# Splitting fp32 operands on ScalarE straight from PSUM, gates by tanh, and a three-pass product with W^T, in a gated GNN followed by graph attention

## The chip, the core and the metric

The kernel runs on one core of a Trainium2 chip. The metric is the device time of that core in microseconds, the median of several runs. The core has a matrix engine (TensorE, PE in the profile; PEld is its weight load), a vector engine (VectorE, DVE), a scalar engine (ScalarE, ACT), GpSimd (POOL) and a queue that issues transfers (SyncE, SP). Matmuls write to PSUM, eight banks of 128 x 512 fp32; everything else is in SBUF.

## The reference

There are 64 graphs of 256 nodes with 256 features. Each graph has its own 256 x 256 adjacency matrix. Two layers are computed:

```
h  = relu(layernorm(x))                 # layer 0
for i in 0..2:
    aggr = A^T (h weight[i])            # A = (adj != 0)
    gi, gh = aggr w_ih^T + b_ih, h w_hh^T + b_hh
    r, z = sigmoid(i_r + h_r), sigmoid(i_z + h_z)
    n = tanh(i_n + r * h_n)
    h = (1 - z) * n + z * h
x  = x + h
h  = relu(layernorm(x))                 # layer 1
g  = h W^T
e  = leaky(g a_left [rows] + g a_right [columns]); masked where adj == 0
x  = x + softmax(e) g
```

## The kernel before, in words

Two graphs make a pair, and there are 32 pairs. The features of a pair lie as two tiles of 128 features x 512 (two graphs of 256 nodes), so the moving operand of a gate matmul is 128 x 512. Each pair goes through three GRU steps (i = 0, 1, 2) and then the attention.

**Precision by splitting.** The gate products are done in float32r, which keeps fewer mantissa bits than fp32. Both operands are split: a value v into a top part v0 (the leading bits) and a remainder v1, and a third tile d that combines the two. The weights' three factors are made once in the setup, by `factors`, into `fac` tiles (`hh` for w_hh; 0, 1, 2 for weight[i] w_ih^T). The moving operands are split at each step by `split` (L445): a VectorE operation that masks off low bits into a fp32 tile t (the cut, L322), a ScalarE copy of t to float32r (L449), a VectorE subtraction v - t (L450), and a VectorE scalar_tensor_tensor for d (L451).

**A gate** (L455) takes one PSUM bank. Its top part adds two float32r products per operand block (L464). ScalarE then scales the bank by 1 + 1/4096 and adds a bias (L478), and the rest adds the third product (L469). A step has six gates: r, z (each from h and from the aggregate), nh (from h) and ni (from the aggregate), each for two blocks of 128 outputs. That is 72 matmuls a step, 216 a pair.

**A step.** The state hT is split into h0, h1. The propagation with A, prop (L584), is eight matmuls of 128 x 256 for each feature block. ScalarE copies its bank into SBUF (L588), and `split` makes g from the copy. Then come the gates: r and z by ScalarE's sigmoid (L599, L610), u = nh * r (L603), u += ni (L606), n by tanh (L607), and h = n + z * (h - n) by three VectorE operations (L615 to L617). For the next propagation h goes back to node-major form by a DMA transpose and a gather on SP (L489, L494), a ScalarE copy that joins 16-bit halves (L502), and a split into hi and lo (L641, L642). In the last pair TensorE transposes instead (L631).

**Attention.** After a second layernorm and relu, the two dot products with a are taken on VectorE (L656) by va, a W prepared in the setup. One of them is spread over the columns by TensorE (L667), Prelu makes the leaky scores (L671), a predicated copy masks them (L674), and a reduction takes the maximum (L676). The four exp instructions of both graphs follow as one operation (L683). The weights are turned by DMA as above (L705, L706; by TensorE in the last pair, L700). Then mix (L714) multiplies them with the features in plain fp32, ScalarE copies the bank to SBUF (L718), and project (L723) multiplies with W^T, plain fp32, four matmuls of 128 x 256 a graph. VectorE divides by the softmax sum and adds the residual (L728), and SP stores (L731).

**The order.** The order of instructions on each engine is written out by a planner (`Plan`) when the kernel is built. Every operation has an engine, an assumed duration, the tiles that it reads and writes, and a priority from a due time less a hand-set lead (`LEAD`, by operation name). The planner places one operation after the other by the time at which it could start, then by priority. Tiles come from slot classes (28 "full", 32 "round", 8 "bank" and so on), and an operation that needs a new tile must wait for a free slot. At most four pairs are in work at once. Each engine works in its order; semaphores keep the dependencies.

Of the kernel before, what the change touches and what calls it, by code (L numbers as in the profile page):

```python
# [27 lines left out]
    "w load": 28000, "w copy": -12000, "w cut": -5000, "w 1": -17000, "w copies": -7000, "G": -9000, "G copy": -5400,  # L28
    "va copy": 4000, "in 0 stats": 5000, "in 1 relu": 10000, "turn copy 0": -11800, "h0 0": 17000, "h0 d": 13000,
    "h1 0": 36000, "prop 0": 11200, "g0 cut": 3000, "g1 cut": 13000, "g1 0": -28000, "r 0 topT": 51000,  # L30
    "r 0 rest": -4300, "r 0": 29000, "ni 0 rest": 46000, "z 0 topF": -48000, "z 0": 11000, "d mul 0": -19000,
    "r 1 topT": -34000, "r 1 rest": -1000, "nh 1 topF": -42000, "nh 1 scale": -38000, "nh 1 rest": 3000,
    "ni 1 topF": -24000, "tanh 1": 10000, "z 1 topF": -61000, "z 1 scale": -112000, "z 1": 6000, "back 0": -36000,
    "hi 0": 28000, "back copy 1": -67000, "hi 1": 52000, "mid 0 stats": -14000, "right 0": -8000,
    "mid 1 eps": -23000, "mid 1 relu": 9000, "dot 1": -31000, "mix 0": -28000, "p copy 1": 40000,
    "project 1": -6000, "turn 1 gather": 2000,
# [16 lines left out]
class Plan:  # L53
# [6 lines left out]
    def __init__(self, window, lead):  # L60
        self.ops, self.slots, self.window, self.pair = [], {}, window, -1
        self.writer, self.readers = {}, {}
        self.due = None
        self.stage = None
        self.lead = lead
        self.keep = {"full": 0, "round": 0}
# [4 lines left out]
    def op(self, name, eng, occ, lat, fn, r=(), w=(), ahead=0, port=False):  # L71
# [3 lines left out]
        o.stage, o.name, o.lead = self.stage, name, self.lead.get(name, 0)  # L75
# [125 lines left out]
def tile_gated_gnn_then_gat(  # L201
# [34 lines left out]

    nc = tc.nc
# [16 lines left out]
    plan.slot_class("full", [const.tile([P, GN], F32, name=f"full{i}") for i in range(28)])  # L254
# [37 lines left out]
    C = 1.0 / SPLIT  # L292

# [4 lines left out]
    b_rz = const.tile([P, EB], F32, name="b_rz")  # L298
    b_i = vec[:, 2 * DB : 2 * DB + EB]
# [3 lines left out]
    wT = const.tile([P, DB, D], F32, name="wT")  # L303
# [21 lines left out]
    def setup():  # L325
# [16 lines left out]
        dve("b_rz", 70, lambda: nc.vector.tensor_add(b_rz, b_i, b_h), r=[("vec", ONE)], w=[("b_rz", ONE)])  # L342

# [10 lines left out]
        def transposed(dst, region, blocks):  # L354

            def go_for(c):
                pt = Buf("bank")

                def go():
                    for r, (b, k) in enumerate(blocks):  # L360
                        nc.tensor.transpose(pt.t[:, ts(r, P)], parts(b)[:, k, ts(c, P)], ident)

                n = len(blocks)
                pe("w turn", TR * n, go, r=[(b, ONE) for b, _ in blocks] + [("ident", ONE)], w=[(pt, ONE)])
                act("w copy", 140 + n * 110, lambda: nc.scalar.copy(dst(c), pt.t[:, : n * P]), r=[(pt, ONE)], w=[region(c)])

            for c in range(DB):
                go_for(c)

        H = E3 // 2  # L370

        def factors(m, T):

            def one(kb, half):
                f = lambda j: fac[m][:, j, kb, ts(half, H)]
                b, t = T[kb][half], Buf("full")
                src, top = lambda: b.t[:, :H], lambda: t.t[:, :H]
                key = (f"fac{m}", ((kb, half),))
                cut("w cut", top, src, H, [(b, ONE)], [(t, ONE)])
                dve2("w 1", 460, lambda: nc.vector.tensor_sub(src(), src(), top()), r=[(t, ONE)], w=[(b, ONE)])  # L380

                def copies():
                    nc.scalar.copy(f(0), top())
                    nc.scalar.activation(f(1), src(), AF.Copy, scale=SPLIT)

                act("w copies", 800, copies, r=[(b, ONE), (t, ONE)], w=[(f"fac{m}", ((kb, half, 0),))])
                dve2("w d", 510, lambda: nc.vector.scalar_tensor_tensor(f(2), top(), -C, src(), op0=ALU.mult, op1=ALU.add),
                    r=[(b, ONE), (t, ONE)], w=[(f"fac{m}", ((kb, half, 1),))])

            for half in range(2):  # L390
                for kb in range(DB):
                    one(kb, half)
# [4 lines left out]
        def whole(T, blocks):  # L397
            for half in range(2):
                transposed(lambda c, half=half: T[c][half].t[:, :H], lambda c, half=half: (T[c][half], ONE),
                           blocks[3 * half : 3 * half + 3])  # L400
# [4 lines left out]
        whole(whhT, whh_n)  # L405
# [24 lines left out]
        transposed(lambda c: wT[:, c, :], lambda c: ("wT", (c,)), W_n)  # L430
# [12 lines left out]
    WT = [("wT", (0, 1))]  # L443

    def split(name, v):  # L445

        t, v0, v1, vd = Buf("full"), Buf("round"), Buf("round"), Buf("round")
        cut(name + " cut", lambda: t.t, lambda: v.t, GN, [(v, ALL)], [(t, ONE)])
        act(name + " 0", C512, lambda: nc.scalar.copy(v0.t, t.t), r=[(t, ONE)], w=[(v0, ONE)])  # L449
        dve2(name + " 1", V512, lambda: nc.vector.tensor_sub(v1.t, v.t, t.t), r=[(v, ALL), (t, ONE)], w=[(v1, ONE)])  # L450
        dve2(name + " d", V512, lambda: nc.vector.scalar_tensor_tensor(vd.t, v1.t.bitcast(F32), -SPLIT, t.t, op0=ALU.mult, op1=ALU.add),  # L451
            r=[(v1, ONE), (t, ONE)], w=[(vd, ONE)])
        return v0, v1, vd

    def gate(name, e, terms, tops, apart=False, bias=0.0):  # L455
# [22 lines left out]
        act(name + " scale", 575 if "nh" in name else A512, lambda: nc.scalar.activation(bank.t, bank.t, AF.Identity, bias=bias, scale=1.0 + C),  # L478
# [4 lines left out]
    def dma_turn(name, src, t, gathers):  # L483
# [5 lines left out]
        plan.op(name, "SP", 1370, 3500, lambda: nc.sync.dma_start_transpose(  # L489
# [6 lines left out]
        for region, dst, blocks in gathers:  # L496
            plan.op(name + " gather", "SP", 1320, 4300 if blocks == slice(None) else 3100, lambda dst=dst, blocks=blocks: gather(dst, blocks),
                    r=[(t, ALL)], w=[region])
# [10 lines left out]
    def norm_relu(name, src, dst):  # L509
# [11 lines left out]
        dve(name + " stats", 995, stats, r=[(src, ALL)], w=[(sm, (0, 1))])  # L521
# [13 lines left out]
    def pair(p):  # L535
        plan.pair = p

# [33 lines left out]
        for i in range(L):  # L571
# [4 lines left out]
            for db in range(DB):  # L576
                pa, ag = Buf("bank"), Buf("full")
# [10 lines left out]
                act(f"prop copy {db}", A512, lambda pa=pa, ag=ag: nc.scalar.copy(ag.t, pa.t), r=[(pa, ONE)], w=[(ag, ALL)])  # L588
                gs.append(split(f"g{db}", ag))
# [5 lines left out]
            for db in range(DB):  # L595
# [3 lines left out]
                act(f"r {db}", 575, lambda b=r_, k=pr, db=db: nc.scalar.activation(b.t, k.t, AF.Sigmoid, bias=b_rz[:, db : db + 1]),  # L599
                    r=[(pr, ONE), ("b_rz", ONE)], w=[(r_, ONE)])  # L600
                en = 2 * DB + db
                ph = gate(f"nh {db}", en, [("hh", hs)], tops, bias=b_h[:, en : en + 1])
                dve(f"u {db}", V512, lambda u=u, k=ph, b=r_: nc.vector.tensor_mul(u.t, k.t, b.t),  # L603
                    r=[(ph, ONE), (r_, ONE)], w=[(u, ONE)])
# [6 lines left out]
                    b.t, k.t, AF.Sigmoid, bias=b_rz[:, DB + db : DB + db + 1]),  # L611
# [4 lines left out]
                dve2(f"d mul {db}", V512, lambda d=d, b=z_: nc.vector.tensor_mul(d.t, d.t, b.t), r=[(z_, ONE)], w=[(d, ALL)])  # L616
                dve2(f"d add {db}", V512, lambda u=u, d=d: nc.vector.tensor_add(d.t, d.t, u.t), r=[(u, ONE)], w=[(d, ALL)])  # L617
# [31 lines left out]
        for g in range(G):  # L649
# [20 lines left out]
            for nb in range(NB):  # L670
                act(f"leaky {g}", 365, lambda b=sc[g], nb=nb, pR=pR, sm=sm: nc.scalar.activation(  # L671
                    parts(b)[:, nb, :], pR.t[:, :N], AF.Prelu, bias=sm.t[:, 12 + nb : 13 + nb], alpha=LEAKY_SLOPE),
                    r=[(pR, ONE), (sm, (12 + nb,))], w=[(sc[g], (nb,))])
# [5 lines left out]
        def exps():  # L679
            for g in range(G):  # L680
                s = sms[g].t
                for k in range(NB):
                    nc.scalar.activation(parts(pm_[g])[:, k, :], parts(pm_[g])[:, k, :], AF.Exp, bias=s[:, k : k + 1],  # L683
                                         accum_out=s[:, 4 + k : 5 + k])

        plan.op("exps", "ACT", 4 * 490 + 2600, 4 * 490 + 1300 + 200, exps, r=[(s, ONE) for s in sms],
                w=[(b, ALL) for b in pm_] + [(s, (1,)) for s in sms])

        for g in range(G):
# [3 lines left out]
            pT, pg, ag, pv = Buf("full"), Buf("bank"), Buf("full"), Buf("bank")  # L693
# [24 lines left out]
            act(f"mix copy {g}", A512, lambda ag=ag, pg=pg: nc.scalar.copy(ag.t, pg.t), r=[(pg, ONE)], w=[(ag, ONE)])  # L718

            def project(ag=ag, pv=pv):  # L720
                for ib in range(NB):
                    for db in range(DB):
                        nc.tensor.matmul(pv.t[:, ts(ib, D)], ag.t[:, db * N + ib * P : db * N + (ib + 1) * P],  # L723
                                         wT[:, db, :], start=(db == 0), stop=(db == DB - 1))

            pe(f"project {g}", 4 * MM, project, r=[(ag, ONE)] + WT, w=[(pv, ONE)])
# [41 lines left out]
```

## Time and profile before

| what | value |
| --- | --- |
| median of 3 runs | 2126.16 us (2124.05 to 2127.03) |
| profiled execution | 2126.64 us |
| its span, first to last instruction | 2124.9 us |
| mean granted TensorE clock | 0.991 |
| L464 and L469 (gates) | 6912 matmuls |
| L584 (prop) | 1536 matmuls of 256 columns |
| L714 (mix), L723 (project) | 512 records each, for 256 instructions |
| table loads on ScalarE | 65, 1283 ns each |
| L502 (join), ScalarE | 310 copies, 1172 ns |
| L478 (gate scale), ScalarE | 768, 592 or 665 ns |

How to read the profile: a row of the groups names line, engine, operation, output<-input by tile names, shapes and count; then the busy time of the group, the mean of one in ns, and the idle time of the engine just before its members with what ended it. A matmul's mean is longer than the distance between two starts, since matmuls overlap. The chain is the work that ended last, followed back from the end: at each point what released the next piece. "issue" is time in which nothing visible was waited for. A wait row reads: engine and line that waited, engine and line waited for, total us, times, longest.

### The profile page before, as it was taken

What the parts mean: (1) busy time and instruction counts of PE and PEld (TensorE: products, weight loads), DVE (VectorE), ACT (ScalarE), POOL (GpSimd) and SP (SyncE); (2) the same over time, 40 slices, a digit from 0 to 9 for tenths busy, and PEclk for the clock granted to TensorE, in tenths of its full rate; (3) what the DMA queues carried; (4) which work ended last, traced back from release to release, by engine and by line L of the source; (5) the groups of instructions that cost most, each with busy time, mean ns of one, the idle gap of its engine ahead of it and who ended that gap; (6) DMA issues with size and microseconds to landing.
All of it is one profiled execution on the core that took longest, in us unless ns stands there. A gap on an engine that the chain in (4) does not pass through costs nothing.

```text
span 2124.9 us, 31090 instructions
## 1 busy us (share of the span) xinstructions
PE 2084.8 (98%) x9737; PEld 1712.9 (81%) x9737; DVE 1780.2 (84%) x4148; ACT 1892.6 (89%) x3255; POOL 142.9 (7%) x198
## 2 busy tenths in 40 slices
PE   8999999999999999999999999999999999999997
PEld 6787888888888888888888888888888888888875
DVE  7787888888888888888888888888888888888775
ACT  7788999999998999998999999999999989999865
POOL 1000000000000000000000000000000000000000
PEclk9999999999999999999999999999999999999998
DMA  3456765656765546766546665556765657665531
GB/s 99 75 105 119 139 117 104 103 108 127 135 118 97 107 110 129 134 119 96 109 110 129 132 120 101 104 112 127 134 118 97 108 108 131 130 119 90 91 59 40
DMA packets 729254, 234.35 MB, mean 110 GB/s; under 512 B 660977, under 2 KB 729089, under 8 KB 729089
## 3 DMA queue, kind: packets, MB, share of 16 engines
q1 hardware_dynamic: 729056, 232.36, 58.0%
q8 instruction: 77, 1.26, 0.3%
q14 instruction: 89, 0.72, 0.1%
q10 hardware_dynamic: 32, 0.01, 0.0%
HBM read 52.96 MB, written 16.78 MB: 33 GB/s over the span
## 4 chain that ended last, share of the span: by engine, by line
PE 78%; ACT 9%; DMA 6%; SPq 3%; DVE 2%; issue 2%; ACTq 0%; DVEq 0%
PE bank L464 39%; PE bank L469 19%; PE bank L584 7%; PE bank L714 6%; DMA full<-full 5%; PE bank L723 5%; SPq L494 3%; ACT full L502 2%; ACT bank L478 2%; ACT full L683 1%; ACT round L449 1%; ACT L683 1%; PE bank L421 1%; PE bank L667 1%; ACT full L599 0%
## 5 line engine op out<-in xcount | busy, mean ns | idle before, releaser
L464 PE MATMUL bank<-round,fac 128*128 128x512 f32 x2304 | 624.1, 399 | 1.9 <-ACT round L449 1.7
L464 PE MATMUL bank<-round,fac_hh 128*128 128x512 f32 x2304 | 617.9, 397 | 3.7 <-ACT round L449 3.6
L464 PEld LDWEIGHTS bank<-round,fac_hh 128*128 128x128 f32 x2304 | 432.8, 189 | 105.8 <-ACT round L449 4.8
L464 PEld LDWEIGHTS bank<-round,fac 128*128 128x128 f32 x2304 | 431.9, 189 | 101.8 <-ACT round L449 2.1
L478 ACT ACTIVATE bank<-bank 128x512 f32<-128x512 f32 x576 | 339.6, 592 | 48.3 <-PE bank L464 46.1
L502 ACT COPY full<-full 128x1024 uint16<-128x1024 uint16 x310 | 363.2, 1172 | 20.8 <-DMA full<-full 15.5
L469 PE MATMUL bank<-round,fac_hh 128*128 128x512 f32 x1152 | 356.2, 399 | 2.4 <-ACT bank L478 1.9
L469 PE MATMUL bank<-round,fac 128*128 128x512 f32 x1152 | 356.5, 396 | 0.5 <-ACT bank L478 0.5
L450 DVE TENSOR_TENSOR round<-full,full 128x512 fp32r<-128x512 f32 x384 | 255.2, 684 | 1.7
L469 PEld LDWEIGHTS bank<-round,fac 128*128 128x128 f32 x1152 | 214.4, 188 | 51.1 <-ACT bank L478 2.9
L469 PEld LDWEIGHTS bank<-round,fac_hh 128*128 128x128 f32 x1152 | 208.4, 189 | 57.6 <-ACT bank L478 16.6
L451 DVE SCALAR_TENSOR_TENSOR round<-round,full 128x512 fp32r<-128x512 f32 x384 | 252.2, 682 | 0.9 <-PE bank L464 0.5
L449 ACT CAST round<-full 128x512 fp32r<-128x512 f32 x384 | 239.5, 631 | 8.5 <-DVE full L322 5.6
L603 DVE TENSOR_TENSOR full<-bank,full 128x512 f32<-128x512 f32 x192 | 131.8, 687 | 114.2 <-ACT full L599 107.9
L524 POOL TENSOR_TENSOR small<-small,nhalf 128x2 f32<-128x2 f32 x128 | 106.2, 839 | 1787.7 <-DVE small L522 1785.5
L584 PEld LDWEIGHTS bank<-round,round 128*128 128x128 f32 x1536 | 206.1, 190 | 17.9 <-DVE round L642 2.7
L584 PE MATMUL bank<-round,round 128*128 128x256 f32 x1536 | 217.2, 287 | 3.4 <-DVE round L642 1.9
L610 ACT ACTIVATE full<-bank,b_rz 128x512 f32<-128x512 f32 x192 | 131.7, 687 | 88.8 <-PE bank L469 88.7
L615 DVE TENSOR_TENSOR full<-full,full 128x512 f32<-128x512 f32 x192 | 132.2, 689 | 75.2 <-ACT full L607 71.9
L322 DVE TENSOR_SCALAR full<-full 128x512 int32<-128x512 int32 (+1 forms) x400 | 163.7, 418 | 17.2 <-ACT full L588 8.8
L616 DVE TENSOR_TENSOR full<-full,full 128x512 f32<-128x512 f32 x192 | 131.8, 688 | 42.6 <-ACT full L610 41.9
L478 ACT ACTIVATE bank<-bank,vec 128x512 f32<-128x512 f32 x192 | 127.7, 665 | 13.1 <-PE bank L464 13.0
(78 smaller groups left out, 2407.6 us busy)
## 6 DMA issues: line engine op xcount, KB each, us to landing
full<-full SPq DMA_DIRECT2D x496, 128.0 KB, 3.5
x<-in_x_dram SPq DMA_DIRECT2D x64, 256.0 KB, 3.3
adj<-in_adj_dram SPq DMA_DIRECT2D x64, 256.0 KB, 3.1
full<-in_x_dram SPq DMA_DIRECT2D x64, 256.0 KB, 3.0
out_dram<-full SPq DMA_DIRECT2D x64, 256.0 KB, 2.4
full<-full SPq DMA_DIRECT2D x248, 64.0 KB, 2.2
full<-full SPq DMA_TRANSPOSE x310, 3.1
full<-in_L_gnn_w_ih_dram SPq DMA_DIRECT2D x3, 256.0 KB, 2.8
```

What stands on the lines that cost most here:

```text
L322: dve2(name, 60 + n * 0.54, lambda: nc.vector.tensor_scalar(dst().bitcast(I32), src().bitcast(I32), CUT, None, op0=ALU.bitwise_and), r=r, w=w)
L449: act(name + " 0", C512, lambda: nc.scalar.copy(v0.t, t.t), r=[(t, ONE)], w=[(v0, ONE)])
L450: dve2(name + " 1", V512, lambda: nc.vector.tensor_sub(v1.t, v.t, t.t), r=[(v, ALL), (t, ONE)], w=[(v1, ONE)])
L451: dve2(name + " d", V512, lambda: nc.vector.scalar_tensor_tensor(vd.t, v1.t.bitcast(F32), -SPLIT, t.t, op0=ALU.mult, op1=ALU.add), r=[(v1, ...
L464: nc.tensor.matmul(bank.t, f(m, j, kb), b.t, start=(first and n == 0), stop=True, skip_group_check=True)
L469: nc.tensor.matmul(bank.t, f(m, 2, kb), s[kb][2].t, start=False, stop=True, skip_group_check=True)
L478: act(name + " scale", 575 if "nh" in name else A512, lambda: nc.scalar.activation(bank.t, bank.t, AF.Identity, bias=bias, scale=1.0 + C), ...
L502: act(name, 1065, lambda: nc.scalar.copy(dst.t.bitcast(U16).rearrange("p (j n b) -> p j n b", j=2, b=2), src.t.bitcast(U16).rearrange(f"p ...
L584: nc.tensor.matmul(pa.t[:, ts(g, N)], b, parts(A[g])[:, sb, :], start=(n == 0), stop=(n == len(terms) - 1))
L603: dve(f"u {db}", V512, lambda u=u, k=ph, b=r_: nc.vector.tensor_mul(u.t, k.t, b.t), r=[(ph, ONE), (r_, ONE)], w=[(u, ONE)])
L615: dve2(f"d sub {db}", V512, lambda u=u, d=d: nc.vector.tensor_sub(d.t, d.t, u.t), r=[(u, ONE)], w=[(d, ALL)])
L616: dve2(f"d mul {db}", V512, lambda d=d, b=z_: nc.vector.tensor_mul(d.t, d.t, b.t), r=[(z_, ONE)], w=[(d, ALL)])
```

## The change

- **Split without a cut.** `split` no longer masks bits into a tile t. ScalarE multiplies v by 1 - 1/8192 and rounds to float32r in one pass, giving v0; VectorE subtracts v0 from v, then makes d from v0 and v1. For g the source is the PSUM bank of the propagation itself, so the ScalarE copy to SBUF is gone, and the bank is read by ScalarE and then by VectorE.
- **r and z by tanh.** sigmoid(y) = (1 + tanh(y/2)) / 2. The factors of one half go into scaled biases, into the n rows of w_hh (halved as they are copied in the setup) and into VectorE operations that become scalar_tensor_tensor.
- **Project in float32r.** W^T gets three factors in the setup. The mix bank is split as g is. Project becomes eight float32r matmuls, a ScalarE scale of its bank, and four more.
- **exps** becomes one planner operation for each graph.
- **Planner.** The slots of class full go from 28 to 26. The leads are other ones, the first and the last pair may have their own, and a few assumed durations are changed.

```diff
-    "project 1": -6000, "turn 1 gather": 2000,
...
+    "right 0": -20000, "dot 1": 9000, "p copy 1": -65000, "c1 d": -31000, "last h0 0": 10000, "last dot 1": -17000,
...
-    plan.slot_class("full", [const.tile([P, GN], F32, name=f"full{i}") for i in range(28)])
+    plan.slot_class("full", [const.tile([P, GN], F32, name=f"full{i}") for i in range(26)])
...
+    BELOW = 1.0 - C / 2
...
-    wT = const.tile([P, DB, D], F32, name="wT")
+    fac["W"] = const.tile([P, 3, DB, D], F32R, name="fac_W")
...
-    def split(name, v):
-
-        t, v0, v1, vd = Buf("full"), Buf("round"), Buf("round"), Buf("round")
-        cut(name + " cut", lambda: t.t, lambda: v.t, GN, [(v, ALL)], [(t, ONE)])
-        act(name + " 0", C512, lambda: nc.scalar.copy(v0.t, t.t), r=[(t, ONE)], w=[(v0, ONE)])
-        dve2(name + " 1", V512, lambda: nc.vector.tensor_sub(v1.t, v.t, t.t), r=[(v, ALL), (t, ONE)], w=[(v1, ONE)])
-        dve2(name + " d", V512, lambda: nc.vector.scalar_tensor_tensor(vd.t, v1.t.bitcast(F32), -SPLIT, t.t, op0=ALU.mult, op1=ALU.add),
-            r=[(v1, ONE), (t, ONE)], w=[(vd, ONE)])
+    def split(name, v, bank=False):
+
+        v0, v1, vd = Buf("round"), Buf("round"), Buf("round")
+        act(name + " 0", A512 if bank else C512, lambda: nc.scalar.activation(v0.t, v.t, AF.Copy, scale=BELOW), r=[(v, ALL)], w=[(v0, ONE)])
+        (dve if bank else dve2)(name + " 1", V512, lambda: nc.vector.tensor_sub(v1.t, v.t, v0.t.bitcast(F32)),
+                                r=[(v, ALL), (v0, ONE)], w=[(v1, ONE)])
+        dve2(name + " d", V512, lambda: nc.vector.scalar_tensor_tensor(
+            vd.t, v1.t.bitcast(F32), -SPLIT, v0.t.bitcast(F32), op0=ALU.mult, op1=ALU.add),
+            r=[(v0, ONE), (v1, ONE)], w=[(vd, ONE)])
...
-                act(f"prop copy {db}", A512, lambda pa=pa, ag=ag: nc.scalar.copy(ag.t, pa.t), r=[(pa, ONE)], w=[(ag, ALL)])
-                gs.append(split(f"g{db}", ag))
+                gs.append(split(f"g{db}", pa, True))
...
-                act(f"r {db}", 575, lambda b=r_, k=pr, db=db: nc.scalar.activation(b.t, k.t, AF.Sigmoid, bias=b_rz[:, db : db + 1]),
+                act(f"r {db}", 575, lambda b=r_, k=pr, db=db: nc.scalar.activation(
+                    b.t, k.t, AF.Tanh, bias=b_rz[:, db : db + 1], scale=0.5),
...
-                dve(f"u {db}", V512, lambda u=u, k=ph, b=r_: nc.vector.tensor_mul(u.t, k.t, b.t),
-                    r=[(ph, ONE), (r_, ONE)], w=[(u, ONE)])
+                dve(f"u {db}", S512, lambda u=u, k=ph, b=r_: nc.vector.scalar_tensor_tensor(
+                    u.t, b.t, 1.0, k.t, op0=ALU.add, op1=ALU.mult), r=[(ph, ONE), (r_, ONE)], w=[(u, ONE)])
...
-                dve2(f"d mul {db}", V512, lambda d=d, b=z_: nc.vector.tensor_mul(d.t, d.t, b.t), r=[(z_, ONE)], w=[(d, ALL)])
-                dve2(f"d add {db}", V512, lambda u=u, d=d: nc.vector.tensor_add(d.t, d.t, u.t), r=[(u, ONE)], w=[(d, ALL)])
+                dve2(f"d mul {db}", V512, lambda d=d, b=z_: nc.vector.scalar_tensor_tensor(
+                    d.t, b.t, 1.0, d.t, op0=ALU.add, op1=ALU.mult), r=[(z_, ONE)], w=[(d, ALL)])
+                dve2(f"d add {db}", V512, lambda u=u, d=d: nc.vector.scalar_tensor_tensor(
+                    d.t, d.t, 0.5, u.t, op0=ALU.mult, op1=ALU.add), r=[(u, ONE)], w=[(d, ALL)])
...
-        plan.op("exps", "ACT", 4 * 490 + 2600, 4 * 490 + 1300 + 200, exps, r=[(s, ONE) for s in sms],
-                w=[(b, ALL) for b in pm_] + [(s, (1,)) for s in sms])
+            act(f"exps {g}", 2 * 497, exps, r=[(sms[g], ONE)], w=[(pm_[g], ALL), (sms[g], (1,))])
...
-            act(f"mix copy {g}", A512, lambda ag=ag, pg=pg: nc.scalar.copy(ag.t, pg.t), r=[(pg, ONE)], w=[(ag, ONE)])
-
-            def project(ag=ag, pv=pv):
-                for ib in range(NB):
-                    for db in range(DB):
-                        nc.tensor.matmul(pv.t[:, ts(ib, D)], ag.t[:, db * N + ib * P : db * N + (ib + 1) * P],
-                                         wT[:, db, :], start=(db == 0), stop=(db == DB - 1))
-
-            pe(f"project {g}", 4 * MM, project, r=[(ag, ONE)] + WT, w=[(pv, ONE)])
+            cs = split(f"c{g}", pg, True)
+
+            def project(js, first, cs=cs, pv=pv):
+                for n, (ib, db, j) in enumerate((ib, db, j) for ib in range(NB) for db in range(DB) for j in js):
+                    nc.tensor.matmul(pv.t[:, ts(ib, D)], cs[j].t[:, db * N + ib * P : db * N + (ib + 1) * P],
+                                     fac["W"][:, j, db, :], start=(first and n == 0), stop=True, skip_group_check=True)
+
+            pe(f"project {g}", 8 * PROP, lambda project=project: project((0, 1), True),
+               r=[(cs[0], ONE), (cs[1], ONE), ("facW", ((0, 0), (1, 0)))], w=[(pv, ONE)])
+            act(f"project {g} scale", A512, lambda pv=pv: nc.scalar.activation(pv.t, pv.t, AF.Copy, scale=1.0 + C), w=[(pv, ONE)])
+            pe(f"project {g} rest", 4 * PROP, lambda project=project: project((2,), False),
+               r=[(cs[2], ONE), ("facW", ((0, 1), (1, 1)))], w=[(pv, ONE)])
```

## The prediction, made before the result was known

> **What bounds the kernel now.** I read the page's busy line first, then the busy time in three stretches, then TensorE's waits in the middle stretch, then the rows that give the price of one instruction, then the chain that ended last. Busy line of the page and the three stretches (columns: length, then PE, PEld, DVE, ACT, POOL busy, granted clock, DMA share, GB/s):
>
> ```profile
> PE 2084.8 (98%) x9737; PEld 1712.9 (81%) x9737; DVE 1780.2 (84%) x4148; ACT 1892.6 (89%) x3255; POOL 142.9 (7%) x198
> ...
> 0.00:200.00 200.00, 185.54 (x818) 145.93 (x819) 153.88 (x343) 162.42 (x292) 14.51 (x26) 0.96 0.51 105
> 200.00:2000.00 1800.00, 1790.73 (x8446) 1480.51 (x8445) 1546.39 (x3613) 1647.39 (x2816) 125.37 (x168) 1.00 0.61 115
> 2000.00:2125.00 125.00, 108.55 (x476) 86.51 (x474) 79.94 (x194) 82.83 (x149) 3.00 (x4) 0.92 0.30 55
> ```
>
> TensorE is busy 1790.7 of the middle 1800 us; it idles 9.3 us there, 14.5 us in the head and 16.5 us in the tail. A busy TensorE need not be at its peak, so I checked by counting: the middle holds 6094 gate matmuls (L464 and L469), at 216 a pair 28.2 pairs, 63.8 us a pair. A pair's work at the pitches read below is 216 x 0.2325 (gates, start to start in the timeline) + 48 x 0.118 (prop, L584) + 32 x 0.217 (mix and project records) + 4 x 0.11 (L667) = 63.3 us. So TensorE runs at its own pace, and ScalarE (91%) and VectorE (86%) are slack there. Its waits in the middle:
>
> ```profile
> PE bank L714 <- ACT full L502: 7.8, 14, 1.3
> PE bank L469 <- ACT bank L478: 1.0, 3, 0.5
> ```
>
> Only 9 us can be won by ending waits in the middle; the rest must come out of TensorE's work, or of head and tail.
>
> **The price rows.** From the groups with shapes kept apart (busy us, mean ns), from the timeline (start us, us), and from the chain (start us, us):
>
> ```profile
> L723 PE MATMUL bank<-wT,full 128*128 128x256 f32 x512 | 115.9, 379 | 0.0
> L588 ACT COPY full<-bank 128x512 f32<-128x512 f32 x192 | 113.5, 591 | 4.8 <-PE bank L584 4.6
> L322 DVE TENSOR_SCALAR full<-full 128x512 int32<-128x512 int32 x384 | 158.7, 420 | 12.8 <-ACT full L588 8.8 <-ACT full L502 3.4
> L603 DVE TENSOR_TENSOR full<-bank,full 128x512 f32<-128x512 f32 x192 | 131.8, 687 | 114.2 <-ACT full L599 107.9 <-PE bank L469 4.3 <-ACT bank L478 0.9
> L683 ACT ACT_TABLE_LOAD x32 | 41.1, 1283 | 0.6
> L599 ACT ACT_TABLE_LOAD x31 | 39.8, 1283 | 1.4 <-PE bank L469 0.8
> ```
>
> ```profile
> 1013.83 1.11 PE L584 MATMUL bank<-round,round 128*128 128x256 f32 x8
> 1014.77 0.63 PE L469 MATMUL bank<-round,fac 128*128 128x512 f32 x2
> ```
>
> ```profile
> 37.40 1.28 ACT L599
> ...
> 66.14 0.67 DVE full L322 x2
> ...
> 2080.37 1.28 ACT L683
> ...
> 2083.77 1.28 ACT L599
> ...
> 2116.89 3.47 PE bank L723 x16
> ```
>
> Mean durations of matmuls overlap, so the pitch is taken from start to start: eight 256-column float32r matmuls take 1014.77 - 1013.83 = 0.94 us, 118 ns each; sixteen project records take 3.47 us, 217 ns each. Each plain float32 project matmul shows as two records (512 for 256 instructions), so 434 ns.
>
> **The change, part by part.**
>
> *Project in three passes, on TensorE.* Out: 16 records a pair x 217 ns = 3.47 us. In: 2 graphs x 12 float32r matmuls of 128 x 256 x 118 ns = 2.83 us. Saved 0.64 us a pair, x 32 pairs = 20.5 us, all of it on the bounding engine. This is the sum's largest term. The Trainium skill, page "TensorE: Matmul & The Clock Gate", section "Back-to-back issue gap", gives N/2.4 + 2.5 ns for an isolated warm matmul: 109 ns at 256 columns, with which the term would be 32 x (3.47 - 24 x 0.109) = 27 us. The row says 118 ns for the same operand kinds and shape, so I take 20.5. From the other side: if alternating operands or accumulation into one bank cost what the L584 group shows as busy per record (217.2 us over 1536, 141 ns), the new matmuls cost 3.39 us and the term is 3 us.
>
> *New waits inside project.* Before, project waited for one ScalarE copy. Now it waits for a ScalarE pass and then a VectorE subtraction, and its last third waits for a scale on ScalarE. In the changed order of instructions I summed the pitches that TensorE has between the end of a mix and its project: median 2.8 us. Needed: 0.17 (a gate matmul lasts 0.399 us at a pitch of 0.2325) + 0.60 + 0.69 + two hand-overs of 0.05 as the chain's issue pieces have them, about 1.6 us, if both queues are free. Between project's first part and its rest lie 1.4 us, about 0.9 needed. Between gate tops and rests the median falls from 2.3 to 1.9 us, and the lowest tenth stays at 1.4; in before such distances cost TensorE 1.0 us in 1800. What would stand behind a late project is the next gates, since TensorE's queue is in order. I take nothing, with a bound of 0.4 us a pair (13 us) above; below, the 7.8 us behind L714 may vanish, since exps no longer wait for two table loads and feed the turn sooner.
>
> *ScalarE.* Out per pair: two table loads 2.57, six prop copies 3.55, two mix copies 1.22. In: two splitting passes and two scales, 2.4 us by the L588 and L478 rows (591, 592 ns); the splits themselves trade one 631 ns cast for one pass. About -5.0 us of 58.3 (1647.4 / 28.2), so ScalarE falls to near 85%. In the middle this is worth nothing: TensorE isn't waiting for it. Where the chain runs through ScalarE it counts: three table loads lie on it, at 37.4, 2080.4 and 2083.8. 3 x 1.28 = 3.85 us. tanh and exp share one set, and the changed instruction list has a single table load. The Trainium skill, "ScalarE: Activation LUTs", section "What ACT_TABLE_LOAD costs", adds about 1.38 us of drain to each switch; that would make 8.0 us. The table loads' rows show 2.0 us of idle in all before 63 loads, so I keep 3.85.
>
> *VectorE.* Out per pair: 12 cuts x 0.420 = 5.04. In: four operations x 0.683 (L450, L451) = 2.73. The rewritten u and d operations become scalar_tensor_tensor; that form costs 682 ns at L451 against 684 to 689 for the plain products, so nothing. A rule that speaks against the change stands in the Trainium skill, "VectorE: DVE Perf Modes", section "Rules for kernel authors": it advises copying a matmul's output to SBUF first if many operations follow, since PSUM operands lose modes. L603 reads PSUM at 687 ns and L615 reads only SBUF at 689, so the subtraction from PSUM costs nothing more here. On the chain the cuts go: 52.6 (0.34), 54.2 (0.34), 66.1 (0.67), 68.0 (0.34), 68.9 (0.34), 2067.1 (0.67), 2.70 us together. In their place a ScalarE pass with its hand-over (0.68) now comes ahead of the subtraction at three spots: +2.04. Net -0.7, between -2.7 and 0.
>
> *PSUM held longer.* A prop or mix bank was free after a copy; now it is held through the subtraction too, about 0.7 us more plus queueing. On TensorE the same bank is next written at least 4.1 us after a prop in the new order (1.6 needed), so nothing.
>
> *Setup and end.* Setup gains W's three factors: by the 384-column rows at L322, L380, L387, L383, L384 at most 2.9 us VectorE and 1.3 us ScalarE (less the two copies to wT). In the new order they stand behind the last layer's factors, where gates of the first pair hide them; uncovered they would cost some 2 us. At the very end project follows mix directly. Before: 3.47 us for both graphs. After, counted from the end of the second mix: first part of graph 0 0.94, graph 1's split ends at 0.17 + 0.60 + 0.69 + 0.1 = 1.6, its first part at 2.5, scale at 3.3, rest at 3.8. +0.3. Head and tail leads are changed as well; the orders show no large move, so 0, with 5 us either way.
>
> POOL and the DMAs do the same work; SP issues as many (950 rows in both).
>
> **Sum.** The profiled execution took 2126.64 us (span 2124.9 and 1.7 around it), 0.5 above the median of 2126.16. 2126.6 - 20.5 - 3.85 - 0.7 + 0.3 = 2101.9, or 2102 us.
>
> **Rivals.**
>
> *Looser helpers pay as well.* ScalarE and VectorE lose 5.0 and 2.3 us a pair, the waits behind L714 end (-7.8), and head and tail close up by some 2 to 5 us. For: 31 us of TensorE's idle lies in head and tail. Against: most of that is dependency, not load. 2102 - 7.8 - 2 = 2092.
>
> *Project stalls a little.* Half a dozen new hand-overs a pair with about 0.5 us to spare; 0.4 us a pair lost is 13 us, 2115. For: the changed order leaves 1.4 us between first part and rest. Against: gates live with such distances.
>
> *The three passes save no TensorE time.* At the 141 ns of the other bound only 3 us of 20.5 are saved: 2119.5. For: busy per record. Against: the timeline's 118.
>
> *Slower: the subtraction from PSUM is stuck behind a waiting VectorE instruction.* VectorE works in order; L603 waits 107.9 us for ScalarE's r over 65 waits, 1.66 each. If such a wait stands ahead of the two mix subtractions and of one prop subtraction of a pair, each overruns its 1.2 us of slack by 0.46 us: 1.4 us a pair, 44 us, giving 2146. It decides the sign from 24.7 / 32 = 0.77 us a pair on. Against: the lowest tenth of the prop distances is 2.3 us, the median 10.7, and VectorE gets freer.
>
> **How the numbers follow.** Likeliest 2102, within 2096 to 2108: 0.60. Looser helpers, 2088 to 2096: 0.17. Small stalls, 2108 to 2116: 0.13. No saving on TensorE, 2116 to 2122: 0.04. Stuck subtraction: 0.06, half of it within 0.2% of before. A measurement of this kernel tells about 0.2% (4.3 us) from no change, so faster 0.93, same 0.04, slower 0.03. The range 2089 to 2114 leaves out about 0.15.
>
> **What would show it.** Project's group: 768 records, pitch near 118 ns, and about 21 us less TensorE busy in all. One table load. ScalarE near 85% and VectorE near 83% of the middle, TensorE still over 99% of it. If waits of project or gate rests on ScalarE or VectorE add up to more than a few us in the middle, the stall rival is right; if project's pitch is over 135 ns, the third is. A pair period well off 63.2 us (63.8 - 0.64), or head and tail moved by more than 5 us, would make the sum wrong.

## The result, and the profile after

The changed kernel takes 2093.58 us (median of 4 runs, 2092.74 to 2095.15) against 2126.6 before (of 4 runs too): ratio 0.9848, 95% interval 0.9831 to 0.9865, or 33 us less. The forecast was 24.7 us less: right in sign, and with the measured time inside its range. Its likeliest time, 2102 us, was 8.4 us too long.

The busy line of the page after:

```profile
PE 2058.8 (98%) x9993; PEld 1702.0 (81%) x9993; DVE 1740.3 (83%) x3900; ACT 1762.2 (84%) x3069; POOL 136.3 (7%) x198
```

The three stretches after (length, then PE, PEld, DVE, ACT, POOL busy, clock, DMA share, GB/s):

```profile
0.00:200.00 200.00, 189.06 (x870) 149.94 (x871) 155.85 (x344) 161.81 (x292) 16.54 (x28) 0.98 0.50 106
200.00:2000.00 1800.00, 1795.75 (x8781) 1492.88 (x8781) 1526.56 (x3416) 1548.72 (x2684) 116.22 (x166) 1.00 0.64 116
2000.00:2091.00 91.00, 74.00 (x346) 59.13 (x344) 57.85 (x141) 51.66 (x95) 3.58 (x4) 0.92 0.23 47
```

TensorE is busy 1795.8 of the middle 1800 us, as before. ScalarE fell from 1647 to 1549 us, VectorE from 1546 to 1527, and TensorE didn't use the room. TensorE's waits between 200 and 1970 us, the whole answer below its heading:

```profile
PE bank L735 <- ACT full L522: 4.2, 14, 0.9
```

This is mix waiting for the joined copy of the turned weights, as in before (7.8 us there). No wait of project (L743) or of a gate rest (L489) is in the list. The groups of the new parts, and the timeline around the two projects of one pair (start us, us):

```profile
L468 DVE TENSOR_TENSOR round<-bank,round 128x512 fp32r<-128x512 f32 x256 | 175.7, 687 | 26.5 <-ACT round L467 26.5
L467 ACT ACTIVATE round<-bank 128x512 fp32r<-128x512 f32 x256 | 152.8, 597 | 19.4 <-PE bank L605 12.6 <-PE bank L735 6.4
...
L624 DVE SCALAR_TENSOR_TENSOR full<-full,bank 128x512 f32<-128x512 f32 x192 | 131.2, 684 | 36.6 <-PE bank L489 29.7 <-ACT full L619 3.5
...
L467 ACT ACTIVATE round<-full 128x512 fp32r<-128x512 f32 x192 | 122.0, 636 | 10.5 <-DVE full L639 10.3
L743 PE MATMUL bank<-fac_W,round 128*128 128x256 f32 x768 | 112.7, 289 | 0.8 <-ACT bank L748 0.5 <-DVE round L468 0.3
```

```profile
1050.06 1.59 PE L743 MATMUL bank<-fac_W,round 128*128 128x256 f32 x12
1051.49 2.02 PE L484 MATMUL bank<-round,fac 128*128 128x512 f32 x8
1053.35 0.63 PE L743 MATMUL bank<-fac_W,round 128*128 128x256 f32 x4
1053.82 0.63 PE L489 MATMUL bank<-round,fac_hh 128*128 128x512 f32 x2
```

Twelve project matmuls take 1051.49 - 1050.06 = 1.43 us, 119 ns each, and four take 0.47, 118 each. The row's busy time doesn't show the saving (112.7 us, against 115.9 for L723 before): mostly because it counts for each block the end of the last matmul, which overlaps with the next start (1.59 us for the twelve, of which 1.43 pass before the next matmul starts), and the new project stands in three blocks a pair where the old one stood in one. The subtraction from PSUM takes 687 ns and the new form of u 684: the prices of the prediction hold.

**Work and losses.** To see where the 33 us are, I split every run in one way. TensorE's work is the count of gate, prop, mix, project and L667 matmuls, each times its pitch in the prediction: 0.2325 us for a gate matmul, 0.118 for prop, 0.217 for a record of mix or of the plain project, 0.118 for the new project, 0.11 for L667. The loss of a stretch is its length less its work: waits, short gaps, a slow clock, and in the head the setup. The stretches are 0 to 200, 200 to 1900, and 1900 to the end. One profiled execution each; the two of the changed kernel (the second is the control below) differ by 2.8 us in all.

| kernel | span | work | head | middle | tail |
| --- | --- | --- | --- | --- | --- |
| before | 2124.9 | 2025.2 | 51.7 | 16.8 | 31.2 |
| after | 2091.0 | 2004.8 | 42.1 | 14.4 | 29.7 |
| after, control | 2094.0 | 2005.0 | 41.4 | 16.0 | 31.5 |

The work fell by 20.4 us, the losses by 11 to 14, of which 10 are in the head. The work column is made with the prediction's pitches and so doesn't test them. The timeline above does for the new project, and for the plain one the trace of before, where neighbouring starts inside a block of sixteen are 216 ns apart. The period of a pair fits, but less sharply. By counts of gates in the middle (5750 and 5809 in 1700 us) it went from 63.86 to 63.21 us, 0.65 less, where 0.64 was forecast; the control's 5802 give 0.57. And 0.17 us of it are fewer waits of TensorE (8.5 us in the 1700 before, 4.0 after). So the largest term holds in TensorE's work, and most of the surplus over the forecast is in the head. There the kernel before had a dip at 150 to 175 us:

```profile
150.00:175.00 25.00, 22.57 (x92) 17.17 (x91) 21.10 (x56) 21.47 (x39) 2.07 (x2) 0.86 0.76 122
```

```profile
150.00:175.00 25.00, 25.00 (x134) 21.41 (x133) 22.20 (x48) 22.97 (x41) 3.13 (x4) 1.00 0.89 165
```

The first line is before, the second after: the idle and the slow clock (0.86) are gone. By an estimate from the two lines that is 6 of the head's 10 us: 2.4 of idle, and 0.14 x 25 = 3.5 by the clock.

### The profile page after: what moved, and what is told of

Its sections match the earlier page's. It is cut to its first block, busy times and chain, and to the rows that moved or that the text cites. A ratio compares the mean times of both kernels' runs of the same rounds, so it can differ in the third digit from the quotient of the medians.

```text
span 2091.0 us, 30965 instructions
## 1 busy us (share of the span) xinstructions
PE 2058.8 (98%) x9993; PEld 1702.0 (81%) x9993; DVE 1740.3 (83%) x3900; ACT 1762.2 (84%) x3069; POOL 136.3 (7%) x198
## 3 DMA queue, kind: packets, MB, share of 16 engines
q1 hardware_dynamic: 729056, 232.36, 60.7%
## 4 chain that ended last, share of the span: by engine, by line
PE 88%; ACT 5%; DMA 4%; SPq 2%; DVE 1%; issue 1%; DVEq 0%; ACTq 0%
PE bank L484 46%; PE bank L489 23%; PE bank L605 7%; PE bank L735 4%; PE bank L743 4%; DMA full<-full 3%; ACT full L522 1%; SPq L514 1%; ACT full L705 1%; ACT bank L498 1%; PE bank L690 1%; PE bank L439 1%; ACT round L467 1%; ACT full L619 0%; ACT full L628 0%
## 5 line engine op out<-in xcount | busy, mean ns | idle before, releaser
L484 PE MATMUL bank<-round,fac 128*128 128x512 f32 x2304 | 616.0, 395 | 0.4 <-DVE round L468 0.2
L484 PE MATMUL bank<-round,fac_hh 128*128 128x512 f32 x2304 | 608.9, 396 | 3.9 <-ACT round L467 2.6
L489 PE MATMUL bank<-round,fac_hh 128*128 128x512 f32 x1152 | 353.0, 400 | 0.8 <-ACT bank L498 0.8
L489 PE MATMUL bank<-round,fac 128*128 128x512 f32 x1152 | 347.2, 395 | 0.1
L470 DVE SCALAR_TENSOR_TENSOR round<-round,round 128x512 fp32r<-128x512 f32 x448 | 301.7, 685 | 3.4
L489 PEld LDWEIGHTS bank<-round,fac 128*128 128x128 f32 x1152 | 214.0, 188 | 50.3 <-ACT bank L498 0.7
L489 PEld LDWEIGHTS bank<-round,fac_hh 128*128 128x128 f32 x1152 | 200.3, 188 | 40.9 <-ACT bank L498 8.5
L468 DVE TENSOR_TENSOR round<-bank,round 128x512 fp32r<-128x512 f32 x256 | 175.7, 687 | 26.5 <-ACT round L467 26.5
L636 DVE TENSOR_TENSOR full<-full,full 128x512 f32<-128x512 f32 x192 | 132.4, 690 | 62.9 <-ACT full L628 62.5
L631 ACT ACTIVATE full<-bank,b_rz 128x512 f32<-128x512 f32 x192 | 131.4, 684 | 44.8 <-PE bank L489 40.9
L467 ACT ACTIVATE round<-bank 128x512 fp32r<-128x512 f32 x256 | 152.8, 597 | 19.4 <-PE bank L605 12.6
L624 DVE SCALAR_TENSOR_TENSOR full<-full,bank 128x512 f32<-128x512 f32 x192 | 131.2, 684 | 36.6 <-PE bank L489 29.7
L619 ACT ACTIVATE full<-bank,b_rz 128x512 f32<-128x512 f32 x192 | 131.9, 688 | 33.1 <-PE bank L489 33.1
L627 DVE TENSOR_TENSOR full<-full,bank 128x512 f32<-128x512 f32 x192 | 131.1, 683 | 29.6 <-PE bank L489 29.1
L628 ACT ACTIVATE full<-full,vec 128x512 f32<-128x512 f32 x192 | 138.2, 720 | 20.5 <-DVE full L627 16.4
```

The costliest lines, as they stand in the source:

```text
L467: act(name + " 0", A512 if bank else C512, lambda: nc.scalar.activation(v0.t, v.t, AF.Copy, scale=BELOW), r=[(v, ALL)], w=[(v0, ONE)])
L468: (dve if bank else dve2)(name + " 1", V512, lambda: nc.vector.tensor_sub(v1.t, v.t, v0.t.bitcast(F32)), r=[(v, ALL), (v0, ONE)], w=[(v1, ...
L484: nc.tensor.matmul(bank.t, f(m, j, kb), b.t, start=(first and n == 0), stop=True, skip_group_check=True)
L489: nc.tensor.matmul(bank.t, f(m, 2, kb), s[kb][2].t, start=False, stop=True, skip_group_check=True)
L628: act(f"tanh {db}", 615, lambda u=u, en=en: nc.scalar.activation(u.t, u.t, AF.Tanh, bias=b_i[:, en : en + 1]), r=[("vec", ONE)], w=[(u, ONE)])
L631: act(f"z {db}", 575, lambda b=z_, k=pz, db=db: nc.scalar.activation(b.t, k.t, AF.Tanh, bias=b_rz[:, DB + db : DB + db + 1], scale=0.5), r ...
```

## The experiments

Theory 1: TensorE's work gave 20 us, and lighter ScalarE and VectorE gave the head's surplus. Rival 2: the new leads gave the surplus. The twelve kernels were measured in three groups of four, and each group has its own runs of the kernel before. "Planned" is where the planner's own schedule ends, by its assumed durations, when it writes out that kernel's order; it is 2092.3 us for the kernel before.

| kernel | planned us | median us | before us | ratio (95%) | head / middle / tail loss |
| --- | --- | --- | --- | --- | --- |
| e1 plain fp32 project | 2131.2 | 2147.26 | 2122.48 | 1.0117 (1.0100 to 1.0134) | 49.1 / 39.2 / 32.9 |
| e2 sigmoid | 2170.7 | 2196.44 | 2122.48 | 1.0351 (1.0336 to 1.0367) | 51.4 / 94.8 / 42.5 |
| e3 splits by cut | 2148.1 | 2204.86 | 2122.48 | 1.0392 (1.0375 to 1.0408) | 46.8 / 107.9 / 44.7 |
| e4 leads of before | 2083.7 | 2101.17 | 2122.48 | 0.9900 (0.9885 to 0.9915) | 45.1 / 20.9 / 29.7 |
| e0 changed, control | 2069.3 | 2093.93 | 2123.08 | 0.9859 (0.9844 to 0.9873) | 41.4 / 16.0 / 31.5 |
| e7 project alone | 2189.3 | 2233.23 | 2123.08 | 1.0514 (1.0498 to 1.0530) | 60.7 / 121.8 / 41.4 |
| e8 tanh alone | 2155.4 | 2191.18 | 2123.08 | 1.0317 (1.0299 to 1.0335) | 46.4 / 80.0 / 37.7 |
| e9 splits alone | 2164.3 | 2208.26 | 2123.08 | 1.0399 (1.0383 to 1.0414) | 51.9 / 87.5 / 44.1 |
| s1 changed, searched leads | 2059.6 | 2095.95 | 2124.92 | 0.9865 (0.9840 to 0.9889) | 39.1 / 22.2 / 27.1 |
| s2 before, searched leads | 2081.1 | 2136.23 | 2124.92 | 1.0058 (1.0038 to 1.0078) | 41.7 / 42.5 / 23.5 |
| s3 plain project, searched leads | 2074.5 | 2095.64 | 2124.92 | 0.9864 (0.9846 to 0.9883) | 37.5 / 9.2 / 22.4 |
| s4 tanh in the order of before | 2092.3 | 2123.09 | 2124.92 | 0.9993 (0.9984 to 1.0002) | 48.9 / 14.8 / 30.9 |

TensorE's work is 2025.3 to 2025.5 us in those with a plain project (e1, e8, e9, s2, s3, s4) and 2004.8 to 2005.0 in the others, whatever the total.

**Undoing one part of the changed kernel (e1, e2, e3).** A piece of each edit, in this order:

```diff
-            cs = split(f"c{g}", pg, True)
+            act(f"mix copy {g}", A512, lambda ag=ag, pg=pg: nc.scalar.copy(ag.t, pg.t), r=[(pg, ONE)], w=[(ag, ONE)])
...
-                    b.t, k.t, AF.Tanh, bias=b_rz[:, db : db + 1], scale=0.5),
+                    b.t, k.t, AF.Sigmoid, bias=b_rz[:, db : db + 1]),
...
-            hs = [split(f"h{db}", hT[db]) for db in range(DB)]
+            hs = [cut_split(f"h{db}", hT[db]) for db in range(DB)]
```

> The changed kernel, with project as before: one ScalarE copy of the mix bank and four plain fp32 matmuls a graph. Everything else is as changed, the leads too. Theory 1 (the middle's gain is TensorE work alone): TensorE gets back 0.64 us a pair, 20.5 us, so about 2114, with the middle's period 63.8 us a pair and TensorE over 99% busy there; head and tail stay at the changed kernel's. Rival (project's three passes cost nearly what the plain ones cost, and the gain came from waits that ended): 2094 to 2100.

> The changed kernel, with r and z by sigmoid (with the same number of vector operations, a factor of 2 in place of the add of 1) and the exps of both graphs as one operation, so that the table loads are back, about 65. Theory 1 (the head's extra gain of some 8 us comes from lighter helper engines, table loads first): the loads cost what lies on the chain, four of 1.28 us and one idle of 2.0, some 5 to 8 us: 2099 to 2102, nearly all in head and tail, nothing in the middle. Rival 2 (the gain comes from the new leads and the order that they give): 2094 to 2096.

> The changed kernel, with the splits of h and g as before: a copy of the propagation's bank to SBUF, and a cut on VectorE; only the split of the mix bank stays new. ScalarE gets 3.5 us a pair more and VectorE 5.0. Theory 1 (lighter helpers gave the head's extra gain): the head loses 3 to 6 us, the middle nothing as long as both stay under 92% busy: 2097 to 2100. Rival 2 (leads): 2094 to 2096. If the middle gets slower by over 5 us, the lighter helpers are worth something there too, which the prediction denied.

All three are far off both expectations, and slower than before. The middle lost it: e1 has 25 us more loss there than the changed kernel has, e2 80, e3 93. The middle of e3, and three of TensorE's waits in it:

```profile
200.00:1900.00 1700.00, 1639.72 (x7816) 1341.57 (x7815) 1460.29 (x3364) 1455.16 (x2542) 116.09 (x152) 0.99 0.61 110
```

```profile
PE bank L494 <- ACT round L479: 14.3, 8, 3.4
PE bank L499 <- ACT bank L508: 13.9, 13, 2.6
PE bank L746 <- ACT full L532: 12.0, 13, 1.9
```

ScalarE is busy 1455 of 1700 us (86%) and VectorE 1460 (86%), no more than in kernels that lose 15 us. TensorE idles because gate tops, rests and mixes stand in its queue ahead of what they need. That points at the order, not at the load. The planned lengths say the same: the planner made e1 to e3 longer than the changed kernel by 62, 101 and 79 us, and they took 54, 103 and 111 us more.

**The order alone (e4).** The table of leads of before, the instructions of after:

```diff
-    "w load": 4000, "load": -2000, "w turn": 11000, "w cut": -16000, "w copies": -49000, "va": 21000,
...
+    "w load": 28000, "w copy": -12000, "w cut": -5000, "w 1": -17000, "w copies": -7000, "G": -9000, "G copy": -5400,
...
```

> The changed kernel with the table of leads of before (those of operations that are gone have no effect; the first and last pair have none of their own). All instructions are the changed kernel's; only their order differs. Rival 2 (the new leads gave the head's extra gain of some 8 us): 2100 or more, with the dip near 160 us back. Theory 1 (lighter helpers gave it): within 3 us of the changed kernel, 2093 to 2097.

Ratio 0.9900, against 0.9859 for the control: the new leads are worth 0.41% between two intervals of 0.15% each, some 9 us (4 to 13). Rival 2 has its amount, but not its place: the dip at 160 us did not come back.

```profile
150.00:175.00 25.00, 24.31 (x127) 20.10 (x126) 22.11 (x48) 23.76 (x46) 2.54 (x4) 1.00 0.93 138
```

By the losses, the changed instructions with the old leads have already saved 6.6 of the head's 10 us (51.7 to 45.1); the new leads give 3 to 4 more there and 5 to 6.5 in the middle. So the leads don't explain the dip. But out of the same leads the planner makes another order when the instructions differ, so e4 doesn't show that the lighter instructions closed it. Two runs speak against the removed cuts as the cause. e3 has all cuts of h and g again and no dip there; e9 has none, with the leads of before, and the deepest dip of all:

```profile
150.00:175.00 25.00, 24.93 (x128) 20.87 (x127) 22.77 (x57) 22.52 (x42) 2.24 (x3) 1.00 0.71 122
```

```profile
150.00:175.00 25.00, 18.80 (x81) 14.82 (x80) 18.38 (x41) 23.26 (x41) 2.79 (x4) 0.93 0.83 130
```

The first line is e3, the second e9. And s2, with every instruction of before in another order, loses 41.7 us in the head, as little as the changed kernel. A light head can thus come from the order alone; what closed the dip in the changed kernel stays open.

**The control and the parts alone, with the leads of before (e0, e7, e8, e9).** e7 puts `split(f"c{g}", pg, True)` and the three passes into the kernel before, and takes its full slots from 28 to 26; e8 puts in tanh, and plans exps without the time for table loads; e9 puts in the new `split` for h and g. Of e8:

```diff
-        plan.op("exps", "ACT", 4 * 490 + 2600, 4 * 490 + 1300 + 200, exps, r=[(s, ONE) for s in sms],
+        plan.op("exps", "ACT", 4 * 490, 4 * 490 + 200, exps, r=[(s, ONE) for s in sms],
```

> The changed kernel once more, beside the parts alone, since the kernel before measured 4 us less on the chip of the first four experiments. Both theories: 0.985 of the kernel before, so 2090 to 2095.

> The kernel before, with its leads, and of the change only the three-pass project with the split of the mix bank straight from PSUM. ScalarE gets 1.2 us and VectorE 2.7 us a pair on top of what they had, so about 93% and 90% of the middle. Theory 1 (TensorE's work bounds, and the helpers keep pace): 20 us less than before, ratio about 0.990. Rival (the lighter splits and gates were needed to make room, the parts only pay together): the middle's losses grow, and ratio 0.995 to 1.02.

> The kernel before, with its leads, and of the change only r and z by tanh (the one half that belongs to nh is put into the add of u instead of into w_hh), so no table loads but the first. ScalarE loses 2.6 us a pair. Theory 1 (TensorE's work bounds; only loads on the chain count, four of 1.28 us and one idle of 2.0): 4 to 7 us less than before, ratio 0.997 to 0.998, nothing of it in the middle. Rival (ScalarE's load in the middle counts): over 10 us less, ratio under 0.995.

> The kernel before, with its leads, and of the change only the splits of h and g by one scaled rounding pass, g straight from PSUM. ScalarE loses 3.6 us and VectorE 5.0 us a pair. Theory 1: 0 to 4 us less than before, ratio 0.998 to 1.000, all of it in head and tail. Rival (PSUM held longer and a subtraction that waits in VectorE's queue): slower than before, ratio over 1.002, with new waits of gate tops on L450's subtraction in the middle.

The control came out as expected. Each part alone is 3 to 5% slower than before, though e8 and e9 only take work away. e9's middle, and its largest waits of TensorE:

```profile
200.00:1900.00 1700.00, 1652.48 (x7635) 1349.41 (x7634) 1304.30 (x2970) 1426.62 (x2398) 113.00 (x153) 0.99 0.58 110
```

```profile
PE bank L471 <- ACT bank L480: 24.1, 24, 1.8
PE bank L715 <- ACT full L504: 11.5, 10, 1.8
PE bank L586 <- ACT round L642: 6.7, 5, 1.4
...
PE bank L466 <- DVE round L450: 0.6, 2, 0.4
```

VectorE has fallen to 77% and ScalarE to 84% here, and still gate rests (L471) wait 24.1 us for their scale, and mix for its join. A subtraction from PSUM that comes late (L466 waiting for L450), the mechanism of the prediction's slower rival, costs 0.6 us. In e7 the rests wait 37.8 us for their scale. The planner had made e7, e8 and e9 97, 63 and 72 us longer than before; they took 110, 68 and 85 us more. So these six kernels don't price the parts. They price an order that doesn't fit its instructions. For e8 and e1 the next runs show it; for the other four it is inferred from the planned lengths and the waits. In e3 and e7 the two slots fewer may have a share, which no run separates.

**The same order, one part changed (s4); and fresh orders (s1, s2, s3).** s4 is e8 with the planned duration of exps left alone (`-` is e8, `+` is s4). In the traces its instructions on TensorE, ScalarE, VectorE and GpSimd stand in the order of before, but for the loads that are gone and one small operation of the setup; its planned length is that of before too.

```diff
-        plan.op("exps", "ACT", 4 * 490, 4 * 490 + 200, exps, r=[(s, ONE) for s in sms],
+        plan.op("exps", "ACT", 4 * 490 + 2600, 4 * 490 + 1300 + 200, exps, r=[(s, ONE) for s in sms],
```

> The kernel before with r and z by tanh, as in the experiment with tanh alone, but with the exps' planned duration left as it was, so that every engine has exactly the order of the kernel before; only the 64 later table loads are gone. Theory 3 (the 70 us that tanh alone lost came from the order and not from tanh): faster than before by 4 to 7 us, as the loads on the chain cost: ratio 0.997 to 0.998, nothing in the middle. Rival (something in the tanh instructions costs): ratio over 1.01.

e8 and s4 have the same instructions; only the planned duration of exps, and with it the order, differs, and they are 68 us apart (2191.2 and 2123.1). This shows that the order did it. Tanh itself is worth 0.7 per mille, 1.5 us (from 3.4 less to 0.4 more), not told apart from nothing, and less than the 4 to 7 us that were expected. The table loads are gone (the row of s4, with its idle before):

```profile
L366 ACT ACT_TABLE_LOAD x1 | 1.3, 1283 | 2.0 <-issue 2.0
```

But what was next in line is just as late. The two longest of TensorE's waits in s4 between 40 and 200 us (its lines are one higher than those of before):

```profile
PE bank L465 <- ACT round L450: 5.6, 3, 3.4
PE bank L585 <- DVE round L643: 2.7, 2, 2.5
```

The prop in the dip still waits, now 2.7 us for VectorE's subtraction (1.4 before), and the dip is where it was: TensorE is busy 21.5 of the 25 us, at a clock of 0.86.

For s1 to s3 the table of leads comes from a hill climb over its entries for the shortest plan, separately for the instructions of after, of before, and of e1.

```diff
-LEAD = {
-    "w load": 4000, "load": -2000, "w turn": 11000, "w cut": -16000, "w copies": -49000, "va": 21000,
+LEAD = {
...
```

> The changed kernel with leads from a fresh search (hill climbing over the leads for the shortest plan); no instruction differs, only the order. Theory 3, formed after the first eight runs (the time is TensorE's work plus what the order leaves idle, and an order must be fitted to its own set of instructions): the order still has some 5 to 9 us to give, ratio to before 0.981 to 0.984. Rival (the leads of the changed kernel are at the limit, or a plan fitted closer only fits the planner's assumed durations): 0.986 or more.

> The kernel before with leads from the same kind of search; no instruction differs, only the order. Theory 3: what the new leads gave the changed kernel isn't tied to its instructions, so before gains too, 5 to 11 us, ratio 0.995 to 0.998, in head and tail. Rival (the new order was possible only because ScalarE and VectorE have less to do): ratio 0.999 or more.

> The changed kernel with project in plain fp32 (as in the first experiment) and leads from a search for this set of instructions. Theory 3: the three passes are worth TensorE's 20.5 us less about 5 us for the added hand-overs: 15 to 21 us more than the changed kernel with searched leads, all in the middle, ratio to before 0.988 to 0.992; and its middle loses no more than the changed kernel's. Rival (the 50 us of the first experiment are the worth of the three passes): ratio over 1.005.

s1 is no better than the changed kernel: it lost less in head and tail, and more in the middle. s2 is 11 us slower than before, by 26 us more loss in the middle, although its head and tail are 18 us better. Their plans are 10 and 11 us shorter than those of the changed kernel and of before. So a shorter plan was not a faster kernel in these two: the planner's assumed durations told apart the orders that cost 50 us and more, not these. s3 does what was expected of neither side: with a plain fp32 project it ties with the changed kernel, having 20.4 us more work and 17 to 20 us less loss. Its middle:

```profile
200.00:1900.00 1700.00, 1698.44 (x8026) 1402.41 (x8025) 1367.70 (x3102) 1430.72 (x2464) 115.37 (x163) 1.00 0.62 117
```

It is the only order here that leaves just 9 us in the middle. e1 has the same instructions and slots as s3 and takes 52 us more. So the whole gain over before can also be had without the three passes, by the other parts and an order that fits them. No version beat the changed kernel clearly.

## Why the prediction was right, point by point

The measured time lies in the range, but not in the likeliest band (2096 to 2108, 0.60). It fell into the band of the looser helpers (2088 to 2096, 0.17), whose reasons held only in part: the waits behind the joined copy should have ended and went from 7.8 to 4.0 us between 200 and 1900, and the head did close up, but no run shows that lighter helpers did it. By the prediction's own sign (head or tail moved by more than 5 us) its sum was wrong in the head, by 10 us. Its largest term was right. The total came out in the range because the range was wide enough for one term that was missing.

- **Three passes on TensorE, 20.5 us.** Right as work: the pitch is 118 to 119 ns, and a pair's period fell by 0.57 to 0.65 us, where the term has 0.64; some of that is fewer waits, so the close match is partly luck. The timeline's pitch is 8% above the isolated gap in the Trainium skill's "TensorE: Matmul & The Clock Gate", section "Back-to-back issue gap" (109 ns at 256 columns, with which the term would be 27 us). The rival with 141 ns a matmul is out. No run prices the term as time with the order held. s3 adds a caution: these 20 us of work are saved in every order, but an order found for the longer work was so good that it made them up.
- **New waits inside project, nothing.** Right in the middle: no wait of L743 there.
- **ScalarE and VectorE, nothing in the middle.** Right for this order: the middle's loss fell by no more than 2.4 us. They came to 86% and 85%, near the forecast 85 and 83.
- **Table loads on the chain, 3.85 us.** Mis-sized: s4 gives 1.5 us (from 3.4 less to 0.4 more). Pieces of the chain were subtracted as if nothing were right behind them. I also had overlooked a fourth load on it, with two idle microseconds ahead, in the dip of before:

```profile
167.53 2.03 issue
169.56 1.28 ACT L610
```

  Taking it away did not close the dip, as s4 shows, so counting it would have taken the term further from the measured 1.5 us.
- **Cuts, 0.7 us.** Not measured: e9 was meant to and measured its order. That their removal closed the dip is not shown, and e3 and e9 speak against it.
- **PSUM held longer, nothing.** Right as far as seen: TensorE waited 0.6 us for a subtraction from PSUM even in e9's poor order.
- **The end, 0.3 us more.** About 0.5. From the end of the last mix (2082.72) to the end of project (2086.69) are 3.97 us against 3.47 before. The last part of the chain:

```profile
2079.97 2.75 PE bank L735 x11
...
2082.74 0.61 ACT round L467
...
2083.37 0.70 DVE round L468
...
2084.12 1.11 PE bank L743 x7
...
2085.31 0.59 ACT bank L748
...
2085.94 0.75 PE bank L743 x4
```

  The new hand-overs, split, first part, scale, rest, stand there one after the other with nothing to hide them. The tail's whole loss moved little: 1.5 us less than before in one profile, 0.3 more in the control.
- **Leads, "so 0, with 5 us either way".** This is the term that failed: 9 us (4 to 13), and more of it in the middle (5 to 6.5) than in the head (3 to 4). With the leads of before the kernel is 21.3 us faster than before (18 to 24, e4), against 24.7 in my sum; the new leads make it 29 to 33. I had read that the orders show no large move and took that for no worth.

What stays open: what closed the dip; why the leads of before still suit all parts of the change together (20.9 us of loss in the middle) and none of them alone (80 to 122); and whether an order as good as s3's exists for the three passes. By an estimate from work and losses that would be 2005 + 69 = 2074 us.

## What to carry to other kernels

When one engine runs at its own pace, count its instructions and multiply by the start-to-start pitch: this term came out at 0.57 to 0.65 us a pair where 0.64 was forecast. When a list scheduler makes the order, a part that is added or undone is only priced with the order held fixed (change what an operation emits, not its planned duration); otherwise the order is measured, which made 68 us between e8 and s4, for a part worth 1.5. Read the planned length first: it had already given most of the time that all six slow kernels lost. A lead table is part of the change: run it alone, in both directions. Here it was run in one (e4); the new leads on the instructions of before were not.

## What the runs showed of the hardware that was not expected

ScalarE's rounding pass to float32r takes 597 ns out of PSUM and 636 out of SBUF (the two rows of L467, 256 and 192 of them), so the source in PSUM is also the faster one for ScalarE, by 39 ns. Of the 65 table loads of before, two (the first, and the one in the dip) have 2.0 us of idle ahead of them that nothing in the trace explains; the other 63 have 2.0 us in all. s4 took away 64 of the 65 and won 1.5 us.
